# Starting a two-layer graph-attention and expert kernel: three first blocks interleaved, and no turn without a block between the layers

## The chip, the cores and the metric

One Trainium2 chip, one core of it. The metric is the device time of one execution in microseconds, as the median of several runs. All data are float32.

## The reference

Two layers follow each other. In each, the tokens x (128 graphs of 64 nodes with 256 features, 8192 tokens) go through graph attention inside each graph, and then through eight experts of which each token takes two:

```python
x = x + gnn(layernorm(x), adj)      # Wh = h @ W; e = Wh@a1 + (Wh@a2).T (layer 1: leaky)
                                    # softmax(where(adj > 0, e, -big)) @ Wh, then elu
x = x + experts(layernorm(x))       # top 2 of 8 by the router's logits
# layer 0: experts are 256 -> 256 (gelu) -> 256, and the normalised tokens are added too
# layer 1: experts are 256 -> 512 (relu) -> 256
```

In both layers a token's two expert outputs are weighted by a softmax over the two chosen logits.

## The kernel before

Tokens are cut into 16 blocks of 512 (four tiles of 128 tokens, two graphs each). For each layer and block there are two generators, whose pieces between two yields are called stages here.

- attend (L260 to L367, twelve stages): for layer 1 first the sum of block b's layer 0 results (L267: mid, plus the two expert rows yb of each token with their weights); layer normalisation's statistics (L223 to L233, with a power on GpSimd), its application on ScalarE (L240); transposes to xt (L251) with copies out of PSUM, one on VectorE (L255) and one on ScalarE (L257); the product with the weights (pw, L290), copied to wh by ScalarE (L297); scores (sm, pe), exponentials (L328), transposes of the attention (pp, L339, copied into one of three pT_bd), the product (po, L348) and the block's result xb (L362, L365).
- route (L402 to L513, ten stages): normalisation again (tn), transposes, logits (pl, L419), the largest two (L369 to L386, L445 to L450), weights, the positions of the tokens in the experts' lists (pn, L476; ix, L494), eight indirect writes of 512 token rows to the lists in DRAM (L499, GpSimd's queue), and from the third block of a part on a plan on VectorE (L535) that takes four slots.

A slot is 256 tokens of one expert. It is fetched from the list by SP's queue (xg, L611), its weights too (wc, L653 to L661; the biases come from a table bcat that is written at the start, L203 to L220), then transposed (x: px, L682), multiplied twice (h: ph, L751; y: py, L779), and its rows are scattered by indirect DMAs on GpSimd's queue, for layer 0 to res (L793), for layer 1 added into the output (L822). A part of a layer's blocks ends with every list filled up to whole slots (fill_up, L516) and a last plan of 15 slots. Layer 0 has two parts, so that layer 1 can begin when the first part's slots are done: blocks 0 to CUT - 1 (CUT is 10, L74) and the rest. The loads of a layer 1 block (L833 to L843) read mid and res, and the program lets them be issued only when all of that part's slots have had their y.

The order on SP, TensorE, VectorE and ScalarE is that of the program from L859 on, written out by hand; before that line, and on GpSimd, a scheduler decides. The loop at L894 makes one turn for each entry of blks: in turn t the attention of block t + 1, the routing of block t and four or five slots are interleaved stage by stage, and the first stages of block t + 2. At L861 blks has an empty entry between the layers: one turn attends to no block. Ahead of the loop stand the constants, the two layers' weights gw (L166 to L192: transposes, products with the score vectors, copies by VectorE), the router's weights, layer 0's bias table, the loads of three blocks and five stages. The loop begins with turn -1. Turn 1 makes layer 1's bias table, and turns 1 and 2 write pads into the unused ends of the lists (rest_of_lists, L846).

Of the kernel before, what the change touches and what calls it, by code (L numbers as in the profile page):

```python
# [8 lines left out]
F32 = mybir.dt.float32  # L9
# [7 lines left out]
P = 128  # L17
# [18 lines left out]
def adj_ffn_kernel(  # L36
# [37 lines left out]
    CUT = NB // 2 + 2  # L74
    CAP = N + 2 * SL
    SB = 2 * TB // SL
    LAG = 2
# [36 lines left out]

    ident = const.tile([P, P], F32, name="ident")
# [5 lines left out]
    for g in range(2):  # L121
        r = slice(g * NG, (g + 1) * NG)
        nc.gpsimd.memset(same[r, r], 1.0)
    before = const.tile([P, P], F32, name="before")
# [3 lines left out]
    nhalf = const.tile([P, TT], F32, name="nhalf")  # L128
    nc.gpsimd.memset(nhalf, -0.5)
# [13 lines left out]
    def counted(name, shape, pattern, base, mult):  # L143
        ti = work.tile(shape, I32, tag="adj", name=f"{name}_i")
        nc.gpsimd.iota(ti, pattern=pattern, base=base, channel_multiplier=mult)
        t = const.tile(shape, F32, name=name)
        nc.vector.tensor_copy(t, ti)
        return t

    token2 = counted("token2", [P, NT], [[2 * P, NT]], 0, 2)  # L150
    token = counted("token", [P, NT], [[P, NT]], 0, 1)
    place = counted("place", [P, ST], [[P, ST]], 0, 1)
    places = counted("places", [P, SL], [[1, SL]], 0, 0)
    steps = counted("steps", [P, KS], [[SL, KS]], 0, 0)
    snum = counted("snum", [P, SF], [[1, SF]], 0, 0)

# [4 lines left out]

# [4 lines left out]
    gw = []  # L166
    for l in range(2):
        gw.append(const.tile([P, KD, D + 2], F32, name=f"gw{l}"))
        av = const.tile([P, KD, 2], F32, name=f"av{l}")
# [3 lines left out]
        nc.sync.dma_start(out=av, in_=gnn_a[l])  # L173
        wt = work.tile([P, KD, D], F32, tag="xt", name=f"wt{l}", bufs=2)
        for o in range(KD):
# [5 lines left out]
            nc.vector.tensor_copy(wt[:, o, :], pt)  # L181
        for k in range(KD):
            pa = ps_c.tile([P, 2], F32, tag="a", name=f"pa{l}_{k}")
            for o in range(KD):
# [3 lines left out]
                    rhs=av[:, o, :],  # L188
# [3 lines left out]
            nc.vector.tensor_copy(gw[l][:, k, D : D + 2], pa)  # L192

    rw = []
    for l in range(2):
        t = const.tile([P, KD, E], F32, name=f"rw{l}")
        nc.sync.dma_start(out=t, in_=router[l].rearrange("(k p) e -> p k e", p=P))
        rw.append(t)
    gb2 = const.tile([P, 2, E], F32, name="gb2")
    nc.sync.dma_start(out=gb2[:, 0, :], in_=bg.partition_broadcast(P))  # L200
    nc.sync.dma_start(out=gb2[:, 1, :], in_=gbias.partition_broadcast(P))
# [43 lines left out]
    def transposed(src, tag, ptag, name):  # L245

        xt = work.tile([P, KD, TB], F32, tag=tag, name=f"xt_{name}", bufs=2)
        for k in range(KD):
# [5 lines left out]
            if k % 2 == 0:  # L254
# [591 lines left out]
    def rest_of_lists(l):  # L846

        for e in range(E):
# [3 lines left out]
                in_=pad[:, :, 0 : ROW[l]],  # L852
            )

    tb0 = gather_biases(0)

# [148 lines left out]
```

## Time and profile before

| | |
|---|---|
| median of 3 runs | 1488.62 us (1485.02 to 1490.95) |
| the profiled execution's own time | 1488.33 us |
| its span | 1486.6 us |
| busy: PE, PEld | 1275.2 us (86%), 1088.6 us (73%) |
| busy: DVE, ACT, POOL | 893.7, 661.6, 767.8 us |
| DMA | 315.42 MB, mean 212 GB/s |

PE is TensorE's matmuls, PEld its weight loads, DVE VectorE, ACT ScalarE, POOL GpSimd, SPq the DMA queue of SyncE. The busy slices give an engine's busy share in 40 equal parts of the span in tenths, PEclk the granted clock of TensorE. A line of the timeline has start and duration in us, engine, source line, operation and tiles, a count, and in brackets the idle time before it and what ended it. A line of busy time by stretch has the stretch, its length, and the busy time of PE, PEld, DVE, ACT and POOL (with the number of instructions), then the clock, the DMA share and GB/s.

### The profile page before, as it was taken

What the parts mean: (1) busy time and instruction counts of PE and PEld (TensorE: products, weight loads), DVE (VectorE), ACT (ScalarE), POOL (GpSimd) and SP (SyncE); (2) the same over time, 40 slices, a digit from 0 to 9 for tenths busy, and PEclk for the clock granted to TensorE, in tenths of its full rate; (3) what the DMA queues carried; (4) which work ended last, traced back from release to release, by engine and by line L of the source; (5) the groups of instructions that cost most, each with busy time, mean ns of one, the idle gap of its engine ahead of it and who ended that gap; (6) DMA issues with size and microseconds to landing.
All of it is one profiled execution on the core that took longest, in us unless ns stands there. A gap on an engine that the chain in (4) does not pass through costs nothing. (4 is left out here: it accounts for less than half of the span.)

```text
span 1486.6 us, 22819 instructions
## 1 busy us (share of the span) xinstructions
PE 1275.2 (86%) x6436; PEld 1088.6 (73%) x6436; DVE 893.7 (60%) x3418; ACT 661.6 (45%) x1549; POOL 767.8 (52%) x742
## 2 busy tenths in 40 slices
PE   4566899888889867888889988999889999899996
PEld 3454777777777755777778877788777887688985
DVE  3557777877667747666776666666666654423332
ACT  2443556554656523555544434445434443233332
POOL 3243566655666645355556545556455555534333
PEclk9676999998999979999999999999999999999999
DMA  4274676678676669667778877988778777998863
GB/s 125 87 224 145 197 234 210 219 250 246 214 225 212 217 229 285 206 227 233 255 253 231 231 193 208 268 227 223 208 210 232 199 196 205 239 248 214 225 174 60
DMA packets 267199, 315.42 MB, mean 212 GB/s; under 512 B 41404, under 2 KB 224319, under 8 KB 267073
## 3 DMA queue, kind: packets, MB, share of 16 engines
q1 hardware_dynamic: 222240, 227.80, 50.9%
q0 software_dynamic: 44832, 86.17, 22.1%
q8 instruction: 51, 0.84, 0.2%
q14 instruction: 76, 0.61, 0.1%
HBM read 215.03 MB, written 102.51 MB: 214 GB/s over the span
## 5 line engine op out<-in xcount | busy, mean ns | idle before, releaser
L751 PE MATMUL ph_s<-xT_s,wc_s 128*128 128x256 f32 x1760 | 417.2, 387 | 57.4 <-DVE xT_s L686 41.6
L779 PE MATMUL py_s<-wc_s,hT_s 128*128 128x256 f32 x1760 | 422.8, 391 | 21.7 <-issue 14.8
L751 PEld LDWEIGHTS ph_s<-xT_s,wc_s 128*128 128x128 f32 x1760 | 332.7, 192 | 119.2 <-DVE xT_s L686 57.4
L779 PEld LDWEIGHTS py_s<-wc_s,hT_s 128*128 128x128 f32 x1760 | 334.8, 195 | 68.8 <-issue 17.9
L822 POOL DMA_INDIRECT out_dram<-ys_s,to_s x142 | 223.5, 1574 | 304.9 <-ACT ys_s L819 189.9
L499 POOL DMA_INDIRECT lists<-tn_r,ix_r x256 | 249.6, 975 | 100.5 <-issue 66.3
L759 ACT ACTIVATE hT_s<-ph_s,wc_s 128x256 f32<-128x256 f32 x440 | 183.0, 469 | 184.6 <-issue 88.0
L793 POOL DMA_INDIRECT res<-ys_s,to_s x156 | 159.1, 1020 | 130.2 <-DVE ys_s L787 58.4
L787 DVE TENSOR_TENSOR ys_s<-py_s,wc_s 128x512 f32<-128x512 f32 x149 | 103.0, 691 | 187.4 <-PE py_s L779 182.7
L686 DVE COPY xT_s<-px_s 128x512 f32<-128x512 f32 x149 | 102.4, 687 | 118.3 <-PE px_s L682 118.3
L290 PE MATMUL pw_g<-gw,xt_g 128*128 128x258 f32 x512 | 130.5, 407 | 2.0 <-ACT xt_g L257 1.9
L290 PEld LDWEIGHTS pw_g<-gw,xt_g 128*128 128x128 f32 x512 | 98.6, 202 | 25.6 <-ACT xt_g L257 9.5
L819 ACT ACTIVATE ys_s<-ys_s,cf_s 128x256 f32<-128x256 f32 x142 | 64.1, 498 | 117.7 <-DVE ys_s L787 117.4
L240 ACT ACTIVATE xn_g<-xs,nb_g,rs_g 128x256 f32<-128x256 f32 x128 | 66.4, 589 | 85.5 <-DVE nb_g L238 85.5
L240 ACT ACTIVATE tn_r<-xb_g,nb_r,rs_r 128x256 f32<-128x256 f32 x128 | 66.4, 589 | 70.4 <-DVE nb_r L238 70.4
L682 PE MATMUL px_s<-ident,xg_s 128*128 128x128 f32 x596 | 91.6, 277 | 0.0
L682 PEld LDWEIGHTS px_s<-ident,xg_s 128*128 128x128 f32 x596 | 76.0, 146 | 13.4 <-issue 0.8
L232 POOL TENSOR_TENSOR rs_r<-ve_r,nhalf 128x4 f32<-128x4 f32 x32 | 39.4, 1232 | 86.8 <-DVE ve_r L230 43.8
L348 PE MATMUL po_g<-wh_g,pT_bd 128*128 128x256 f32 x256 | 71.1, 426 | 9.7 <-ACT pT_bd L342 9.5
L339 PE MATMUL pp_g<-ident,ee_g 128*64 128x128 f32 x128 | 22.1, 302 | 61.1 <-DVE ee_g L335 41.0
L297 ACT COPY wh_g<-pw_g 128x258 f32<-128x258 f32 x128 | 48.0, 375 | 59.1 <-PE pw_g L290 58.2
L348 PEld LDWEIGHTS po_g<-wh_g,pT_bd 128*128 128x128 f32 x256 | 52.6, 213 | 23.3 <-ACT pT_bd L342 10.9
(475 smaller groups left out, 1626.3 us busy)
## 6 DMA issues: line engine op xcount, KB each, us to landing
wc_s<-in_w_dram SPq DMA_DIRECT2D x142, 512.0 KB, 4.6
wc_s<-in_w_dram SPq DMA_DIRECT2D x156, 256.0 KB, 3.4
xg_s<-lists SPq DMA_DIRECT2D x78, 258.0 KB, 4.1
xg_s<-lists SPq DMA_DIRECT2D x71, 260.0 KB, 4.3
yb<-res SPq DMA_DIRECT2D x16, 1024.0 KB, 11.1
wc_s<-bcat SPq DMA_DIRECT2D x78, 129.0 KB, 3.9
wc_s<-bcat SPq DMA_DIRECT2D x71, 130.0 KB, 6.2
xs<-in_x_dram SPq DMA_DIRECT2D x16, 512.0 KB, 5.6
```

The source lines that it names most:

```text
L240: nc.scalar.activation(outs(t), xb[:, t, :], AF.Identity, bias=nb[:, t : t + 1], scale=rs[:, t : t + 1])
L290: nc.tensor.matmul(pw, lhsT=xt[:, k, t * P : (t + 1) * P], rhs=gw[l][:, k, :], start=(k == 0), stop=(k == KD - 1),)
L348: nc.tensor.matmul(po[h][:, j, :], lhsT=pT[:, 2 * h + j, :], rhs=wh[:, 2 * h + j, 0:D], start=True, stop=True,)
L499: ins = nc.gpsimd.indirect_dma_start(out=lists[l], out_offset=bass.IndirectOffsetOnAxis(ap=ix[:, k, t : t + 1], axis=0), in_=tn[:, t, 0 : ...
L682: nc.tensor.transpose(px[:, c, t * P : (t + 1) * P], xg[:, t, c * P : (c + 1) * P], ident)
L686: nc.vector.tensor_copy(xT, px)
L751: nc.tensor.matmul(ph[:, j, :], lhsT=wc[:, o : o + P], rhs=xT[:, c, :], start=(c == 0), stop=(c == KD - 1),)
L759: nc.scalar.activation(hT[:, f + j, :], ph[:, j, :], AF.Gelu if l == 0 else AF.Relu, bias=wc[:, OB1[l] + f + j : OB1[l] + f + j + 1],)
L779: nc.tensor.matmul(py[:, t, :], lhsT=hT[:, f, t * P : (t + 1) * P], rhs=wc[:, O2[l] + f * D : O2[l] + (f + 1) * D], start=(f == 0), stop=( ...
L787: nc.vector.tensor_tensor(ys, py, wc[:, OB2[l] : OB1[l]].unsqueeze(1).to_broadcast([P, ST, D]), ALU.add)
L793: ins = nc.gpsimd.indirect_dma_start(out=res[sl["part"]], out_offset=self.row(sl, t), in_=ys[:, t, :], in_offset=None, bounds_check=2 * N - 1,
L822: ins = nc.gpsimd.indirect_dma_start(out=out, out_offset=self.row(sl, t), in_=ys[:, t, :], in_offset=None, compute_op=ALU.add,)
```

## The change

Five things are changed. (1) The hand-written order starts ahead of the constants. SP's queue begins with the first block's x, then gw and the score vectors of layer 0; the rest of the first three blocks' loads and the router's weights follow. Layer 1's gw, layer 0's bias table and the counted constants come at fixed places in a new list of rounds. The copies in make_gw are ScalarE's. (2) In these rounds the attention and routing of blocks 0, 1 and 2 advance side by side, one stage of each in a round; block 3 joins in round 11 and block 4, with its first three stages, in round 20. For blocks 0 to 2 both copies of the transposes are ScalarE's. (3) The loop begins at turn 3. Layer 1's bias table and the pads now stand in turns 3 and 4. (4) blks has no empty entry. The load of layer 1's block 0 stands at the end of the turn two ahead of the boundary; its first stage (the sum), which would come early in the next turn, is left out there and comes together with the second, later in that turn. (5) CUT is 9. The number of slots is the same: 43 and 35 for layer 0's two parts where there were 47 and 31, and 71 for layer 1. The index of pT_bd follows from the missing entry.

```diff
     NB = N // TB
-    CUT = NB // 2 + 2
+    CUT = NB // 2 + 1
     CAP = N + 2 * SL
     SB = 2 * TB // SL
+    FIRST = 3
     LAG = 2
...
+
+    ctx.enter_context(tc.manual_schedule(engines=ORDERED))
     ident = const.tile([P, P], F32, name="ident")
...
-    def counted(name, shape, pattern, base, mult):
-        ti = work.tile(shape, I32, tag="adj", name=f"{name}_i")
-        nc.gpsimd.iota(ti, pattern=pattern, base=base, channel_multiplier=mult)
-        t = const.tile(shape, F32, name=name)
-        nc.vector.tensor_copy(t, ti)
-        return t
-
-    token2 = counted("token2", [P, NT], [[2 * P, NT]], 0, 2)
-    token = counted("token", [P, NT], [[P, NT]], 0, 1)
-    place = counted("place", [P, ST], [[P, ST]], 0, 1)
-    places = counted("places", [P, SL], [[1, SL]], 0, 0)
-    steps = counted("steps", [P, KS], [[SL, KS]], 0, 0)
-    snum = counted("snum", [P, SF], [[1, SF]], 0, 0)
-
...
-    gw = []
-    for l in range(2):
+    gw, av = [], []
+
+    def load_gw(l):
         gw.append(const.tile([P, KD, D + 2], F32, name=f"gw{l}"))
-        av = const.tile([P, KD, 2], F32, name=f"av{l}")
+        av.append(const.tile([P, KD, 2], F32, name=f"av{l}"))
         nc.sync.dma_start(
...
         )
-        nc.sync.dma_start(out=av, in_=gnn_a[l])
+        nc.sync.dma_start(out=av[l], in_=gnn_a[l])
+
+    def make_gw(l):
         wt = work.tile([P, KD, D], F32, tag="xt", name=f"wt{l}", bufs=2)
...
                 )
-            nc.vector.tensor_copy(wt[:, o, :], pt)
+            nc.scalar.copy(wt[:, o, :], pt)
         for k in range(KD):
...
                     lhsT=wt[:, o, k * P : (k + 1) * P],
-                    rhs=av[:, o, :],
+                    rhs=av[l][:, o, :],
                     start=(o == 0),
...
                 )
-            nc.vector.tensor_copy(gw[l][:, k, D : D + 2], pa)
-
-    rw = []
-    for l in range(2):
-        t = const.tile([P, KD, E], F32, name=f"rw{l}")
-        nc.sync.dma_start(out=t, in_=router[l].rearrange("(k p) e -> p k e", p=P))
-        rw.append(t)
+            nc.scalar.copy(gw[l][:, k, D : D + 2], pa)
+
+    rw = [const.tile([P, KD, E], F32, name=f"rw{l}") for l in range(2)]
     gb2 = const.tile([P, 2, E], F32, name="gb2")
-    nc.sync.dma_start(out=gb2[:, 0, :], in_=bg.partition_broadcast(P))
-    nc.sync.dma_start(out=gb2[:, 1, :], in_=gbias.partition_broadcast(P))
+
+    def load_router():
+        for l in range(2):
+            nc.sync.dma_start(out=rw[l], in_=router[l].rearrange("(k p) e -> p k e", p=P))
+        nc.sync.dma_start(out=gb2[:, 0, :], in_=bg.partition_broadcast(P))
+        nc.sync.dma_start(out=gb2[:, 1, :], in_=gbias.partition_broadcast(P))
+
+    def counted(name, shape, pattern, base, mult):
+        ti = work.tile(shape, I32, tag="cap", name=f"{name}_i")
+        nc.gpsimd.iota(ti, pattern=pattern, base=base, channel_multiplier=mult)
+        t = const.tile(shape, F32, name=name)
+        nc.vector.tensor_copy(t, ti)
+        return t
...
-    def transposed(src, tag, ptag, name):
+    def transposed(src, tag, ptag, name, both):
...
                 )
-            if k % 2 == 0:
+            if k % 2 == 0 and not both:
                 nc.vector.tensor_copy(xt[:, k, :], pt)
...
         yield
-        xt = transposed(xn, "xt", "a", name)
+        xt = transposed(xn, "xt", "a", name, l == 0 and b < FIRST)
         yield
...
             nc.tensor.transpose(pp[:, t, :], ee[:, t, :], ident)
-        pT = pT_bd[(NB * l + b + l) % 3]
+        pT = pT_bd[(NB * l + b) % 3]
         nc.vector.tensor_copy(pT[0:NG, :, 0:NG], pp[:, :, 0:NG])
...
         yield
-        tT = transposed(tn, "tT", "r", name)
+        tT = transposed(tn, "tT", "r", name, l == 0 and b < FIRST)
         yield
...
-    def load_block(l, b):
+    def load_block(l, b, first=None):
...
         nc.sync.dma_start(out=xs, in_=(mid_t if l else x_t)[b])
+        if first:
+            first()
         if l:
...
-    tb0 = gather_biases(0)
-
...
-
-    ctx.enter_context(tc.manual_schedule(engines=ORDERED))
     slots = Slots()
-    blks = [{"l": 0, "b": b} for b in range(NB)] + [{}] + [{"l": 1, "b": b} for b in range(NB)]
+    blks = [{"l": l, "b": b} for l in range(2) for b in range(NB)]
...
-    def load(i):
+    def load(i, first=None):
         if there(i):
...
                 assert all(s["l"] or s["part"] != part(k["b"]) for s in slots.all[slots.ny :])
-            k["in"] = load_block(k["l"], k["b"])
+            k["in"] = load_block(k["l"], k["b"], first)
             k["a"] = attend(k["l"], k["b"], k)
...
     h, y, x = slots.h, slots.y, slots.x
-    load(0)
+
+
+    load(0, lambda: load_gw(0))
     load(1)
-    put_biases(0, tb0)
     load(2)
-    a(0, 3)
+    load_router()
+    a(0, 2)
+    make_gw(0)
+    a(0)
     a(1, 2)
-    for t in range(-1, len(blks)):
+    token2 = counted("token2", [P, NT], [[2 * P, NT]], 0, 2)
+    token = counted("token", [P, NT], [[P, NT]], 0, 1)
+    place = counted("place", [P, ST], [[P, ST]], 0, 1)
+    att = lambda b: [(a, b)] * 9 + [(a, b, 2), (a, b)]
+    chains = [
+        (0, att(0)[3:] + [(r, 0)] * 10),
+        (1, att(1)[2:] + [(r, 1)] * 10),
+        (2, att(2) + [(r, 2)] * 10),
+        (11, att(FIRST) + [(r, FIRST)] * 2),
+        (20, [(a, FIRST + 1)] * 3),
+    ]
+    turn = 0
+    while any(c for _, c in chains):
+        for first, chain in chains:
+            if turn >= first and chain:
+                stage, *what = chain.pop(0)
+                stage(*what)
+        if turn == 2:
+            places = counted("places", [P, SL], [[1, SL]], 0, 0)
+            steps = counted("steps", [P, KS], [[SL, KS]], 0, 0)
+            snum = counted("snum", [P, SF], [[1, SF]], 0, 0)
+            tb0 = gather_biases(0)
+        if turn == 5:
+            put_biases(0, tb0)
+            load_gw(1)
+        if turn in (6, 8, 11):
+            load(FIRST + (turn - 6) // 2)
+        if turn == 11:
+            make_gw(1)
+        turn += 1
+    slots.fetch()
+    for t in range(FIRST, len(blks)):
         n = t + 1
         more = slots.nf - slots.ny > SB or len(slots.all) - slots.ny > SB
-        if t >= 0 and t + 3 != NB + 1:
+        if t + 3 != NB:
             load(t + 3)
-        if t == 1:
+        if t == FIRST:
             put_biases(1, gather_biases(1))
             rest_of_lists(0)
-        if t == 2:
+        if t == FIRST + 1:
             rest_of_lists(1)
...
         r(t)
-        if t >= 0:
+        if t + 2 != NB:
             a(t + 2)
...
         y()
-        if t >= 0:
-            a(t + 2)
+        a(t + 2, 1 + (t + 2 == NB))
         if more:
...
         r(t)
-        if t + 3 == NB + 1:
+        if t + 3 == NB:
             load(t + 3)
```

More of the change, by code (lines that the diff above doesn't have):

```diff
@@ L123, in adj_ffn_kernel @@
         nc.gpsimd.memset(same[r, r], 1.0)
+    nhalf = const.tile([P, TT], F32, name="nhalf")
+    nc.gpsimd.memset(nhalf, -0.5)
     before = const.tile([P, P], F32, name="before")
@@ L127, in adj_ffn_kernel @@
     nc.gpsimd.memset(ones, 1.0)
-    nhalf = const.tile([P, TT], F32, name="nhalf")
-    nc.gpsimd.memset(nhalf, -0.5)
     order = const.tile([P, E], F32, name="order")
```

## The prediction

> **What bounds the kernel now.** I read the page's slices first, then the chain that ended last, then busy time in stretches cut where TensorE (it runs in program order) starts a block's first transposes (tile pt_g): 44.1, 69.0, 95.7, 122.8, 150.0, 182.9 us for blocks 1 to 6 of layer 0, then every 31 to 35 us. I call such a stretch a turn.
>
> ```profile
> PE   4566899888889867888889988999889999899996
> PEclk9676999998999979999999999999999999999999
> ```
>
> TensorE is at eight or nine tenths except in the first four slices (150 us), where its granted clock is low too, and in slices 15 and 16 (520 to 595 us), at the boundary of the layers. The chain that ended last has PE products back to back from about 1290 us on:
>
> ```profile
> 1364.09 3.45 PE ph_s L751 x16
> 1368.82 3.46 PE py_s L779 x16
> ```
>
> So the end is a run of expert products without a gap, and their sum is the same in both kernels. A gain can only be TensorE's idle or slow time ahead of it. The stretches (PE, PEld, DVE, ACT, POOL busy, clock, DMA share, GB/s):
>
> ```profile
> 44.10:69.00 24.90, 16.27 (x68) 12.21 (x68) 13.63 (x53) 11.62 (x31) 4.06 (x5) 0.71 0.18 53
> 69.00:95.70 26.70, 17.65 (x68) 13.15 (x68) 15.11 (x63) 11.72 (x31) 11.94 (x13) 0.69 0.81 235
> 95.70:122.80 27.10, 18.04 (x68) 13.38 (x68) 15.24 (x63) 11.78 (x31) 11.84 (x13) 0.69 0.55 166
> ...
> 244.90:275.60 30.70, 27.30 (x150) 23.25 (x149) 24.03 (x96) 17.56 (x40) 18.36 (x20) 1.00 0.71 229
> 444.00:478.60 34.60, 31.35 (x170) 26.80 (x169) 25.54 (x99) 20.97 (x44) 21.25 (x22) 1.00 0.66 206
> 511.30:556.70 45.40, 31.20 (x133) 25.26 (x132) 22.10 (x89) 13.54 (x26) 22.57 (x23) 0.77 0.73 239
> 556.70:597.00 40.30, 30.03 (x142) 24.74 (x141) 27.96 (x96) 16.86 (x35) 21.78 (x23) 0.96 0.98 281
> 597.00:635.70 38.70, 32.68 (x170) 27.70 (x169) 25.70 (x86) 19.37 (x41) 14.43 (x15) 0.96 0.67 212
> 796.60:841.50 44.90, 40.76 (x215) 35.62 (x214) 29.30 (x113) 19.84 (x51) 24.63 (x21) 1.00 0.82 223
> ```
>
> The first three are turns of the start: 25 to 27 us each, 8 to 9 of them idle, clock 0.7: one block after the other, a chain of short steps and no expert product to fill it. Then a layer 0 turn with four expert slots (30.7), with five (34.6): a slot more costs 3.9 us. From 511.3 to 556.7 is the turn without a block: 45.4 us, 31.2 busy, clock 0.77. 556.7 is the turn in which layer 0's last list is filled up (40.3 with no routing in it), 597.0 an ordinary layer 1 turn with five layer 0 slots (38.7), 796.6 one with four layer 1 slots (44.8). In the turn without a block the timeline has this:
>
> ```profile
> 530.19 3.89 DVE L267 SCALAR_TENSOR_TENSOR xs<-yb,cs,xs 128x256 f32<-128x256 f32 x8 [5.87 <-DMA yb<-res]
> 534.74 3.78 PE L779 MATMUL py_s<-wc_s,hT_s 128*128 128x256 f32 x8 [6.52 <-DVE ys_s L787]
> ```
>
> VectorE stands 5.87 us for the landing of layer 1 block 0's yb at the sum L267, then sums for 3.89 us; TensorE gets its next product 6.52 us late and runs it in 3.78 us for 8 matmuls instead of 1.89: its clock has dropped.
>
> [...] L290's 16 matmuls take 5.09 us in the turn at 44.1 and 3.83 at 341.0. [...] finished products wait behind L267 above. So a step placed too early in an engine's order stalls what is behind it, and so will three interleaved chains. [...] The list writes (L499) here land 2.6 to 2.8 us after issue.
>
> **The change, part A: the start.** The order of the built program gives the same slot products done at block 6's first transposes of layer 0 (4), so I compare that moment: 182.9 us before. Added work: nothing on TensorE; 6 copies of 0.69 us of the three blocks and 4 weight copies leave VectorE for ScalarE (0.59 us there), which has room (12 of 27 us busy per turn).
>
> What follows is an estimate. I walked the new order by hand, each step starting when its input and its engine's step before are done, with the trace's durations: statistics 2.3, pow on GpSimd 1.04, normalising 2.1, transposes 2.8 with their wait, pw 3.8 warm to 5.1 cold (I take 4.3), pe 1.1, exponentials 1.4, po 2.0 to 3.7 (2.9), largest 1.3, second largest 1.7, pn and positions 2.7. x now stands first in SP's queue: it lands at about 5 us (13.4 before), its normalising starts at 8.9 (18.5 before). From there chain 0 has its pw at 12.6 to 17.0, exponentials to 24.1, pT at 29.5 (behind block 2's xn on ScalarE), po 30.3 to 33.0, xb at 36.3, statistics to 41.1, tn 45.3 to 47.4 (behind block 2's exponentials), largest at 52.7, second largest at 58.6, pn at 70.7 (in TensorE's order behind block 3's transposes, which wait for its xn), positions (ix) at 73. Alone it is hardly earlier than before (70.7) although it starts ten sooner. But ix of block 1 comes at 83 (97 before) and of block 2 at 91 (124).
>
> Next late is GpSimd. Its order has 8 list writes for each of three blocks and one mid write ahead of the pow of blocks 4 and route 3, and it issues one write in 1.27 us:
>
> ```profile
> 98.81 1.10 POOL L499 DMA_INDIRECT lists<-tn_r,ix_r  x1 [0.28 <-DMA lists<-pad]
> 100.22 0.98 POOL L499 DMA_INDIRECT lists<-tn_r,ix_r  x1 [0.30 <-issue]
> ```
>
> 25 issues after 73 end at 73 + 31.5 = 104.5, the two pows at 106.6; VectorE, with block 2's plan (22 steps of 0.2) and statistics, reaches the same point at 104.3. Block 4's transposes: 106.5, against 122.8. That is 16 us gained.
>
> Part of it goes back. The pads, the second biases and layer 1's bcat stood in turns without slots; now they stand in SP's queue between the first list reads and the first expert weights:
>
> ```profile
> 66.27 1.22 SPq L214 DMA_DIRECT2D tb<-in_b_dram  x1
> 72.90 0.39 SPq L220 DMA_DIRECT2D bcat<-tb  x1
> 92.46 6.03 SPq L850 DMA_DIRECT2D lists<-pad  x8
> ```
>
> List reads from 107 (last write lands) take 3.6 us, xs and adj 1, tb to its landing 7.2 (65.7 to 72.9 above), eight pads 6.0, the first slot's weights 2.1 and landing 5: about 132.5. TensorE would be at the first slot's ph at 106.5 + 21.5 (block 4's po ends so long after its pt_g) = 128. The wait of 4.5 us, cold matmuls after it, two slots and their activations (block 5's xn stands behind them on ScalarE) make this turn 38 us; bounds 30 (weights in time) to 41. The next, with two slots, 28.5 (27.2 with none; 32.8 with four as the first such turn). Block 6: 106.5 + 38 + 28.5 = 173, so A = 9 to 10 us. I take 9. Bounds: 20 if matmuls are warm and weights in time; 0 if matmuls stay cold and the weights come later still.
>
> **Part B: the boundary.** From block 10 of layer 0 (306.4 us; 20 slots done in both) to block 9 of layer 1 (932.9; 94 done in both) before takes 626.5 us. CUT at 9 moves the fill-up one turn earlier at the same cost (37.6 against 30.7 in the turn at 337.1). It makes the turns after it five-slot turns one block sooner; the number of slots stays 78 for layer 0 (43 + 35 for 47 + 31). After: the fill-up turn 37.6; blocks 11 to 15 with five slots 5 x 34.6 = 173.0; layer 1 block 0, now with route 15 and five slots, 38.7; block 1 with the second fill-up 38.7 + 5 = 43.7 (the penalty was 6.9 at 337.1 and some 4 at 556.7); blocks 2 to 4 3 x 38.7 = 116.1; block 5 with one layer 1 slot among five 38.7 + 3.3 = 42.0; blocks 6 to 8 with five layer 1 slots where there were four, 3 x (44.8 + 7.2) = 156.0 (7.2: 3.45 + 3.46 us of products in the chain, and 0.3 of transposes not overlapped). One turn in four had 1.7 more. Sum 608.8. B = 626.5 - 608.8 = 17.7, I take 18. That is the idle of one turn fewer and the stall with its cold matmuls. Cross-check by what goes and comes: 45.4 goes; one more layer 0 slot in a turn (3.9), three more layer 1 slots (21.6) and the fill-up beside a block (3.4) come, 3.1 leave with block 5's turn (42.0 for 45.1): 19.6, less the 1.7.
>
> The sum L267 of block 0 now stands after two products and most of a turn's steps, some 20 us behind its load; yb took 9.8 to 14.9 us to land over the sixteen. I cost it at its 3.9 us alone; with the cover gone it costs 6 to 9 again: behind it on VectorE stand the next xT and ys, and TensorE and GpSimd wait for those. Moving nhalf and the constants, pT_bd's index and the load callbacks cost nothing: GpSimd's memsets end before 7 us, ahead of its first pow. The tail after block 9 has the same order: 0.
>
> **Sum.** The profiled execution took 1488.3 us (span 1486.6, 1.7 around it; the median of the runs is 1488.6, so the same). 1488.3 - 9 - 18 = 1461.
>
> **Rivals.** (1) The start gives more: interleaving keeps TensorE warm and the first weights come in time, A = 20 to 28: 1442 to 1450. For: from 18 to 45 us my walk has PE nearly without gaps. Against: the SP queue above. (2) The start gives nothing: three chains in one FIFO order hold each other up, and GpSimd's 25 issues start at 83: A = -1 to 0, 1471. With part of B lost as well (VectorE stands at L267 again, 6 to 9 us), 1478. For: VectorE is busy only 15 of 27 us before, so rounds are latency, not work. (3) Slower: with five layer 1 slots a turn and no empty turn, yb lands late in every layer 1 turn, 5.87 us of standing and 3 of cold matmuls each as at 530: over nine turns 80, so 1541; it ends slower than before from four such turns on. Against: bytes per us stay (229 GB/s with four slots) and only one of sixteen loads was late before. (4) The empty turn's removal is no gain, as its slots only move: B = 3, A = 9: 1476.
>
> **Chances.** Forecast with A 0 to 20 and B 9 to 21 (1447 to 1479): 0.72. Rival 1: 0.12; 2: 0.09; 4: 0.04; 3: 0.03. Bounds of A and B hardly fall together, so the range is 1445 to 1477, with under 2 in 10 outside (half of rival 1 and of 2, rival 3, the forecast's ends). A measurement tells about 0.5% (7.4 us) from no change; faster by that, below 1481: 0.94 (the forecast and rivals 1, 2 and 4 but their outermost end); same 0.03; slower 0.03 (rival 3).
>
> **What would show it.** Right: block 4's first transposes at 100 to 112 us, gated by rs_g after block 2's list writes; TensorE's first ph waiting for a DMA of wc near 132; block 6 near 173; no DMA wait at the sum L265 (its line after); block 9 of layer 1 some 27 us earlier than 932.9, and the rest equal. Wrong: positions of block 0 after 83 or before 65; a yb wait in turns of layer 1; a five-slot layer 1 turn over 54 us.

## The result, and the profile after

| | before | after |
|---|---|---|
| median of four runs each | 1487.43 us (1485.02 to 1490.95) | 1467.71 us (1464.47 to 1469.72) |
| ratio, with its 95% interval | | 0.9863 (0.9847 to 0.9879) |
| profiled execution, its span | 1488.33, 1486.6 us | 1464.47, 1462.6 us |

The kernel became 1.4% faster: about 20 us by the medians, 24 in the two profiled executions (the profiled one of after is the fastest of its four). The forecast was 1461 with 1445 to 1477: inside the range, with 7 us less gained. Eight of the twelve runs below fell on chips on which the kernel before itself takes 1713 to 1715 us instead of 1487, so their ratios are to the kernel before on their own chip.

The page's slices of the kernel after:

```profile
PE   6646789889989888888889999899988998899996
PEclk9766999989999999999999999999999999999999
```

The dip at slices 15 and 16 is gone. The first four (146 us) still stand at 4 to 6 tenths, with a clock of 7, 6 and 6 tenths from the second on. Busy time by stretch, cut where a block's first transposes start (PE, PEld, DVE, ACT, POOL, clock, DMA share, GB/s):

```profile
9.81:72.06 62.25, 45.37 (x180) 33.75 (x181) 33.20 (x123) 33.91 (x89) 15.04 (x20) 0.82 0.31 88
72.06:111.28 39.22, 18.55 (x77) 14.74 (x77) 23.07 (x117) 12.45 (x33) 26.93 (x28) 0.63 0.27 95
111.28:150.05 38.77, 27.49 (x113) 20.88 (x114) 17.39 (x67) 16.02 (x38) 5.67 (x7) 0.70 0.94 280
150.05:177.16 27.11, 19.27 (x110) 16.24 (x109) 20.35 (x83) 13.17 (x33) 18.01 (x19) 0.97 0.66 213
177.16:210.60 33.44, 30.27 (x148) 24.91 (x149) 24.64 (x103) 20.15 (x44) 17.74 (x19) 0.92 0.61 193
444.60:479.20 34.60, 31.35 (x171) 26.80 (x170) 25.39 (x99) 20.95 (x44) 20.85 (x22) 1.00 0.62 198
479.20:519.70 40.50, 33.59 (x171) 28.40 (x170) 28.91 (x107) 20.96 (x44) 23.14 (x24) 0.92 0.78 263
519.70:557.20 37.50, 31.23 (x170) 26.66 (x169) 29.24 (x108) 21.33 (x45) 22.71 (x24) 1.00 0.81 262
557.20:598.10 40.90, 34.81 (x170) 29.31 (x169) 32.51 (x127) 19.36 (x41) 22.16 (x23) 0.92 0.92 276
755.40:806.60 51.20, 48.13 (x251) 42.01 (x249) 30.46 (x118) 23.46 (x58) 24.75 (x21) 1.00 0.78 227
```

Line by line: the three interleaved blocks (62 us, 45 of them busy); block 3, of which TensorE works only 18.55 of 39.22 us; the turn of block 4 with the first slots; that of block 5; block 6; a five-slot turn (34.6, as before); the turn of layer 0's block 15, 40.5; layer 1's blocks 0 and 1; and a turn with five layer 1 slots (51.2; the forecast had 52.0). Two comparisons, each of one profile of either kernel, show where the time went. At block 6 of layer 0 the same slots are done in both kernels: 177.2 us for 182.9. From block 10 of layer 0 (302.9) to block 9 of layer 1 (909.0) are 606.1 us for 626.5. So the boundary gave 20.4, and the start 5.7 at block 6 and 3.4 at block 10 (302.9 for 306.4). After block 9 both take the same. The start's share did not repeat in the later profiles, as will be seen.

The start, in SP's queue (start, duration, idle in brackets):

```profile
110.99 3.07 SPq L609 DMA_DIRECT2D xg_s<-lists  x4
115.72 2.26 SPq L212 DMA_DIRECT2D tb<-in_b_dram  x1
123.15 0.40 SPq L218 DMA_DIRECT2D bcat<-tb  x1
123.65 9.29 SPq L850 DMA_DIRECT2D lists<-pad  x8
134.15 0.40 SPq L651 DMA_DIRECT2D wc_s<-in_w_dram  x1
143.06 6.41 SPq L850 DMA_DIRECT2D lists<-pad  x8
166.40 5.08 SPq L609 DMA_DIRECT2D xg_s<-lists  x4
```

GpSimd's queue and TensorE in the same stretch:

```profile
77.72 1.11 POOL L497 DMA_INDIRECT lists<-tn_r,ix_r  x1 [5.26 <-DVE cs L466]
79.13 0.98 POOL L497 DMA_INDIRECT lists<-tn_r,ix_r  x1 [0.30 <-issue]
...
108.36 0.96 POOL L497 DMA_INDIRECT lists<-tn_r,ix_r  x1 [0.30 <-issue]
109.34 1.05 POOL L230 TENSOR_TENSOR rs_g<-ve_g,nhalf 128x4 f32<-128x4 f32 x1
110.37 1.00 POOL L230 TENSOR_TENSOR rs_r<-ve_r,nhalf 128x4 f32<-128x4 f32 x1
```

```profile
111.28 2.80 PE L249 MATMUL pt_g<-ident,xn_g 128*128 128x128 f32 x8 [13.60 <-ACT xn_g L238]
...
128.47 3.78 PE L346 MATMUL po_g<-wh_g,pT_bd 128*128 128x256 f32 x8 [1.84 <-ACT pT_bd L340]
138.66 3.38 PE L749 MATMUL ph_s<-xT_s,wc_s 128*128 128x256 f32 x8 [6.40 <-DMA wc_s<-in_w_dram]
```

25 writes follow each other from 77.72 to 109.3 without a break, then come the two pows, and block 4's first transposes had waited 13.60 us for the xn that hangs on the first pow. The list reads at 110.99 are followed by the tables and eight pads that take 9.29 us to issue, and only then by the first weights at 134.15. TensorE had ended block 4's po at 132.25: its first expert product waited 6.40 us and took 3.38 us for eight matmuls, at a granted clock of 0.56 from 138.66 to 141.87; the next two, at 143.25 and 145.09, took 1.99 and 1.89 us at a clock of 1.00. The second eight pads stand in the next turn.

The boundary: the sum (L265) of layer 1's block 0, VectorE and TensorE.

```profile
498.82 3.75 DVE L265 SCALAR_TENSOR_TENSOR xs<-yb,cs,xs 128x256 f32<-128x256 f32 x8
...
504.81 0.68 DVE L684 COPY xT_s<-px_s 128x512 f32<-128x512 f32 x1
505.55 3.78 PE L749 MATMUL ph_s<-xT_s,wc_s 128*128 128x256 f32 x8 [4.90 <-DVE xT_s L684]
```

No line on the sum has a DMA wait any more, in any of the sixteen blocks. But the sum and the statistics behind it keep VectorE for 6 us, the next xT copy stands right behind them, and TensorE waits 4.90 us for it and runs the product in 3.78, at a granted clock of 0.50. Block 15's turn is 40.5 us long where its five-slot neighbours take 34.6.

### The profile page after: what moved, and what is told of

It reads as the page before. It is cut to its first block, busy times and chain, and to the rows that moved or that the text cites. A ratio compares the mean times of both kernels' runs of the same rounds, so it can differ in the third digit from the quotient of the medians.

```text
span 1462.6 us, 22822 instructions
## 1 busy us (share of the span) xinstructions
PE 1264.9 (86%) x6436; PEld 1082.9 (74%) x6436; DVE 885.6 (61%) x3404; ACT 670.3 (46%) x1567; POOL 767.8 (52%) x742
## 5 line engine op out<-in xcount | busy, mean ns | idle before, releaser
L777 PE MATMUL py_s<-wc_s,hT_s 128*128 128x256 f32 x1760 | 417.1, 387 | 14.9 <-issue 14.6
L777 PEld LDWEIGHTS py_s<-wc_s,hT_s 128*128 128x128 f32 x1760 | 331.4, 193 | 59.9 <-issue 17.2
L817 ACT ACTIVATE ys_s<-ys_s,cf_s 128x256 f32<-128x256 f32 x142 | 64.1, 499 | 141.1 <-DVE ys_s L785 134.8
L288 PE MATMUL pw_g<-gw,xt_g 128*128 128x258 f32 x512 | 125.5, 395 | 1.7 <-ACT wh_g L295 1.3
L277 POOL TENSOR_SCALAR cap_g<-adj 128x256 f32<-128x256 int32 x32 | 35.7, 1117 | 91.6 <-DMA adj<-in_adj_dram 90.2
L417 PEld LDWEIGHTS pl_r<-rw,xt_r 128*128 128x128 f32 x512 | 68.1, 207 | 2.9 <-DVE xt_r L253 0.6
```

The source lines that it names most:

```text
L288: nc.tensor.matmul(pw, lhsT=xt[:, k, t * P : (t + 1) * P], rhs=gw[l][:, k, :], start=(k == 0), stop=(k == KD - 1),)
L777: nc.tensor.matmul(py[:, t, :], lhsT=hT[:, f, t * P : (t + 1) * P], rhs=wc[:, O2[l] + f * D : O2[l] + (f + 1) * D], start=(f == 0), stop=( ...
```

## Experiments on chips where the kernel before takes 1487 us

These four ran on one chip with seven runs of the kernel before: 1487.66 us.

**The changed kernel once more.** No edit.

> The changed kernel itself, unchanged, beside the earlier experiments. There the kernel before took 1714 us, and from block 5 on each turn showed TensorE idle for 4 to 10 us while GpSimd wrote list rows and SP read lists. Theory (that idle hits turns with a block and five slots hardest, so the turn taken away is paid back): the boundary alone was at 1.007 of the kernel before, the start alone at 0.999, so both together at 1.003 to 1.007. Rival (the 0.986 of the first measurement holds wherever it is taken, and the edits of the two halves were at fault): 0.986.

1469.21 us, ratio 0.9875 (0.9855 to 0.9896): the first result holds in a second set of runs. The rival's number came; its second half, that the edits of the two halves were at fault, is not tested by it, and neither is the theory, which was about chips of the other kind. Its start is slower than in the first profile though. Same program, same place:

```profile
143.27 3.78 PE L749 MATMUL ph_s<-xT_s,wc_s 128*128 128x256 f32 x8 [11.69 <-DMA wc_s<-in_w_dram]
```

A wait of 11.69 us instead of 6.40. The first weights were issued at 135.46 for 134.15, and the median time from issue to landing of the weights in this stretch was 7.1 us for 4.1. Block 6 came at 182.6, block 10 at 308.9. Block 10 to block 9 of layer 1: 606.7, the same as in the first profile (606.1).

**The sum in three pieces.**

```diff
                         ALU.mult,
                         ALU.add,
                     )
+                if b == 0 and t == 1:
+                    yield
...
-        a(t + 2, 1 + (t + 2 == NB))
+        a(t + 2)
...
         h()
+        if t + 2 == NB:
+            a(NB)
...
         x()
+        if t + 2 == NB:
+            a(NB)
```

> The changed kernel with the sum of layer 1 block 0 and its statistics in three pieces spread over block 15's turn instead of one piece of 6.2 us. Theory (the piece as a whole keeps VectorE from the next xT, TensorE waits 4.9 us for it and runs the next product cold): that wait goes and block 15's turn is 4 to 6 us shorter than the changed kernel's in the same conditions, 0.3% of the time. Rival (the pieces only move the wait to other products): the turn within 1.5 us.

1465.24 us, ratio 0.9851 (0.9830 to 0.9872); its four runs (1463.1 to 1466.1) lie below the four of the unchanged kernel (1467.2 to 1470.9). Block 15's turn takes 37.8 us for 41.3, and block 10 to block 9 is 602.7 us.

```profile
502.71 1.91 DVE L265 SCALAR_TENSOR_TENSOR xs<-yb,cs,xs 128x256 f32<-128x256 f32 x4
504.54 0.68 DVE L686 COPY xT_s<-px_s 128x512 f32<-128x512 f32 x1
505.27 1.95 DVE L265 SCALAR_TENSOR_TENSOR xs<-yb,cs,xs 128x256 f32<-128x256 f32 x4
505.28 1.99 PE L751 MATMUL ph_s<-xT_s,wc_s 128*128 128x256 f32 x8 [0.74 <-DVE xT_s L686]
```

The xT copy now lies between the two halves of the sum, and the product behind it waits 0.74 us and takes 1.99 us for its eight matmuls, where in the first profile of the changed kernel it took 3.78, behind 4.90 us of idle and at a clock of 0.50. The theory is right in kind, and the rival (within 1.5 us) is out; 3.5 us are won instead of 4 to 6. The rest of the turn's excess (37.8 for 34.6) is in part 1.79 us in which a later product waits for its weights.

**Pads early, block 3 and block 4 sooner.**

```diff
-        (11, att(FIRST) + [(r, FIRST)] * 2),
-        (20, [(a, FIRST + 1)] * 3),
+        (7, att(FIRST) + [(r, FIRST)] * 2),
+        (13, [(a, FIRST + 1)] * 3),
...
             put_biases(0, tb0)
+            tb1 = gather_biases(1)
             load_gw(1)
+            rest_of_lists(0)
+            rest_of_lists(1)
+            put_biases(1, tb1)
...
-        if t == FIRST:
-            put_biases(1, gather_biases(1))
-            rest_of_lists(0)
-        if t == FIRST + 1:
-            rest_of_lists(1)
```

> The changed kernel with the pads and layer 1's biases ahead of block 3's load in the start, block 3's chain four rounds sooner and block 4's seven. The earlier runs showed two things: pads just ahead of the list writes hold those up by 6.5 us, and it is the pow of route 3, not only that of block 4, that stands behind the list writes. Theory (these two gates, GpSimd's list writes and SP's pads, set the start): list writes start at 76 to 80, block 4's first transposes stand ahead of 100, the first expert product is at 122 to 127 instead of 138.7, and block 6 is 11 to 16 us earlier than in the changed kernel in the same conditions. Rival (three chains already fill VectorE and ScalarE, so block 3 in their midst delays the first three): list writes after 84, block 6 less than 5 us earlier.

1465.39 us, ratio 0.9852 (0.9830 to 0.9874); the intervals of this run and of the unchanged kernel overlap. Block 6 is at 178.0 for 182.6, 4.6 us sooner. Both numbers of the rival came and none of the theory's (block 4's first transposes are at 107.1, the first expert product at 140.95); of the theory only its second gate, SP's queue, was as it said. GpSimd, VectorE, then TensorE:

```profile
93.92 1.11 POOL L497 DMA_INDIRECT lists<-tn_r,ix_r  x1 [1.15 <-DVE ix_r L492]
...
116.31 0.16 DVE L236 SCALAR_TENSOR_TENSOR nb_r<-mv_r,rs_r 128x4 f32<-128x4 f32 x1 [5.97 <-POOL rs_r L230]
...
123.20 5.62 PE L288 MATMUL pw_g<-gw,xt_g 128*128 128x258 f32 x16 [14.15 <-DVE xt_g L253]
...
137.62 3.49 PE L346 MATMUL po_g<-wh_g,pT_bd 128*128 128x256 f32 x8 [2.00 <-ACT pT_bd L340]
140.95 1.89 PE L749 MATMUL ph_s<-xT_s,wc_s 128*128 128x256 f32 x8
```

The list writes start at 93.92, 16 us later: block 3 among the first three delays them, as the rival said (block 4's statistics, sooner too, may have a part in it). Block 4's product pw then waits 14.15 us, since its xt copy (122.37) stands on VectorE behind route 3's normalisation, which waits 5.97 us for a pow that GpSimd does between list writes, and behind block 2's plan (118.64 to 122.4). But the first expert product, at 140.95, follows po without any wait for weights: without pads and tables in between, the first weights are issued 6.9 us after the last list write ends, where the unchanged kernel on this chip takes 26.3. In spite of list writes 16 us later that product comes 2.3 us sooner.

**List reads one by one.**

```diff
             self.limit = self.nf
+            self.reads()
+
+        def reads(self):
             while self.nf < min(len(self.all), self.ny + 8):
...
             self.ahead()
+            self.reads()
```

> The changed kernel with list reads issued one after each slot's second product instead of five together at a turn's end. Theory (TensorE's idle of 4 to 10 us a turn comes where SP's burst of list reads meets GpSimd's list writes; layer 1 block 1 of the start-alone run, without list writes, had none): the idle shrinks by half or more, 26 turns x 4 to 8 us, 100 to 200 us less than the changed kernel in the same conditions. Rival (the list writes alone do it, or the weights' reads): within 20 us.

1468.87 us, ratio 0.9876 (0.9857 to 0.9895): no difference. It was made against the idle time that the other chips showed (below); on this chip that idle is absent (TensorE's gaps of over 3 us from block 5 to block 9 of layer 1 add up to 13.8 us in the unchanged kernel, where the start-alone run below has 142), so it says only that the burst of five reads costs nothing here. Block 6 at 179.8, block 10 to block 9 607.3 us.

## Experiments on chips where the kernel before takes 1714 us

**The boundary alone.** The kernel before with CUT at 9, no empty entry, and the later sum:

```diff
-    CUT = NB // 2 + 2
+    CUT = NB // 2 + 1
...
-        pT = pT_bd[(NB * l + b + l) % 3]
+        pT = pT_bd[(NB * l + b) % 3]
...
-    blks = [{"l": 0, "b": b} for b in range(NB)] + [{}] + [{"l": 1, "b": b} for b in range(NB)]
+    blks = [{"l": 0, "b": b} for b in range(NB)] + [{"l": 1, "b": b} for b in range(NB)]
...
-        if t >= 0:
+        if t >= 0 and t + 2 != NB:
             a(t + 2)
...
-            a(t + 2)
+            a(t + 2, 1 + (t + 2 == NB))
```

> The kernel before with the boundary's part alone (no turn without a block, CUT at 9, the sum of layer 1 block 0 later). Theory (the two parts are separate, and the boundary carried most of the gain: 20.4 us of 24 in the traces): 1468 us, that is 20 below the kernel before; block 10 of layer 0 still near 306, block 9 of layer 1 near 912, and the turn of block 15 near 40 us with a late product in it. Rival (the parts need each other, since a layer's turns only stay full when the start runs ahead): under 14 us gained.

> The kernel before with the boundary's part alone, once more on another chip if there is one. Theory (the parts are separate, the boundary carries 20.4 of 24 us): ratio to the kernel before 0.986 to 0.987; block 10 of layer 0 near 306, block 9 of layer 1 near 912, and a wait of TensorE of 4 to 6 us in the turn of block 15. Rival (the parts need each other): ratio 0.991 or more.

> The kernel before with the boundary's part alone, on a chip where the kernel before takes 1487 us if this one is such. Theory (the boundary carries 20 us of the gain and the start 0 to 4): ratio 0.985 to 0.989, block 10 of layer 0 near 306, block 9 of layer 1 near 911, a wait of 4 to 6 us for VectorE's xT in block 15's turn. Rival (the parts need each other): ratio 0.991 or more.

Three chips: 1.0065 (1.0045 to 1.0085), 1.0071 (1.0053 to 1.0090), 1.0049 (1.0030 to 1.0068). The boundary alone is slower there, by 9 to 11 us, and the theory missed three times. The rival's number is met, but its reason has no support: with a start beside it, the run with block 4's pow moved (below, its start no faster) is at 1.0041, still slower, and the best kernel with both parts is at 0.9969 there, not at 0.986. The changed kernel itself was not run on these chips. Whether the boundary alone gives its 20 us where the kernel before takes 1487 was not measured either; there it was always run with the start.

**The start alone.** The changed kernel with CUT at 10, the empty entry and the sum's old place put back (the lines above the other way).

> The changed kernel with the turn without a block, CUT at 10 and the sum's old place put back: the start alone. Theory: it gives 3 to 4 us, 1484 to 1485; block 6 near 177 and block 10 near 303. Rival (the start gives the 9 us of the forecast, and the boundary less): 1479. Rival (the start gives nothing and costs, hidden by the boundary): 1488 or more.

0.9988 (0.9968 to 1.0008): at most 5.5 us gained, with zero inside the interval. That leaves room for the theory's 3 to 4 and for nothing, and on this chip not for the forecast's 9. Beside the boundary-alone run on the same chip, which has the old start, block 6 comes later (190.5 for 187.0) and block 10 sooner (350.8 for 355.0).

**Why the boundary costs there.** In the start-alone run, layer 1's block 1 and block 3, TensorE with SP and GpSimd:

```profile
716.90 3.83 PE L288 MATMUL pw_g<-gw,xt_g 128*128 128x258 f32 x16
717.78 3.90 SPq L609 DMA_DIRECT2D xg_s<-lists  x5
```

```profile
796.01 0.96 POOL L497 DMA_INDIRECT lists<-tn_r,ix_r  x1 [0.30 <-issue]
797.20 6.08 SPq L609 DMA_DIRECT2D xg_s<-lists  x5
...
807.33 4.20 PE L288 MATMUL pw_g<-gw,xt_g 128*128 128x258 f32 x8 [7.68 <-issue]
```

In block 1's stretch, right after the turn without a block, no list is written, five list reads take 3.90 us to issue and pw's sixteen matmuls run through; the stretch takes 37.5 us. In block 3's, list writes and list reads meet, the reads take 6.08 us, and pw stands still for 7.68 us in its middle; the stretch takes 48.7. Turns with both show gaps of 3.4 to 9.8 us: from block 5 to block 9 of layer 1, TensorE's gaps of over 3 us add up to 142 us in this run, to 13 in the changed kernel's first profile. The turn without a block is what makes the one stretch without list writes; taking it away takes the one cheap stretch away. In the first profile of before the same stretch has no list writes either, but is not cheap there (38.7 us, the next two 38.7 and 39.4). No run varied it alone, so it is argued, not shown, and it can be only part of the cause. By stretches, in us, with the start-alone and the boundary-alone run of one chip on the right (from block 10 on those two differ in the boundary's edits alone):

| stretch | before, after (1487) | start alone, boundary alone (1714) |
|---|---|---|
| block 10 to block 15 of layer 0 | 172.3, 176.2 | 222.5, 230.5 |
| block 15 to block 2 of layer 1 | 157.1, 119.0 | 177.6, 150.2 |
| block 2 to block 6 of layer 1 | 160.9, 157.2 | 201.2, 202.4 |
| block 6 to block 9 of layer 1 | 136.2, 153.7 | 152.0, 176.9 |
| sum | 626.5, 606.1 | 753.4, 760.0 |

Where the turn is taken away the gain is 27.4 us instead of 38.1; the missing 10.7 are about the cheap stretch (37.5 for 48.7). But the three turns that now do five layer 1 slots instead of four cost 24.9 more instead of 17.5, and the other two rows together lose 9.2 where they lose 0.2 on the 1487 us side. So the loss of the one turn's gain is spread over all stretches, and why fuller turns cost more on these chips stays open.

**Pads in the rounds.** The changed kernel; pads and tables stand in round 11 of the start instead of turns 3 and 4.

```diff
         if turn == 11:
             make_gw(1)
+            put_biases(1, gather_biases(1))
+            rest_of_lists(0)
+            rest_of_lists(1)
```

> The changed kernel with the pads of both lists and layer 1's biases moved from the first two turns into the rounds of the start, ahead of the list writes. Theory (SP's queue sets the first expert weights, as it holds tb, bcat and 16 pads between the first list reads and the first weights): the first weights are issued near 118 instead of 134, the wait of 6.4 us ahead of the first ph goes, and with it the late list reads of the next turn: block 6 at 167 to 171 instead of 177, 1458 to 1462 us. Rival (GpSimd's 25 list writes set it, and TensorE then only waits for the next link): block 6 stays within 2 us of 177 and the time within 2 of the changed kernel.

0.9995 (0.9969 to 1.0020). GpSimd's first list write, and TensorE at block 4's end:

```profile
84.22 1.11 POOL L497 DMA_INDIRECT lists<-tn_r,ix_r  x1 [11.84 <-DMA lists<-pad]
...
134.96 3.55 PE L346 MATMUL po_g<-wh_g,pT_bd 128*128 128x256 f32 x8 [1.84 <-ACT pT_bd L340]
138.35 1.89 PE L749 MATMUL ph_s<-xT_s,wc_s 128*128 128x256 f32 x8
```

The weights are issued at 122.52 for 136.03 in the start-alone run (whose start is the changed kernel's) and no product waits for them: block 6 is at 181.7 for 190.5. The theory's 6 to 10 us are there, and its rival is out; in time it cannot be read off, as the changed kernel was not run beside it (the run below with block 4's pow moved, its block 6 at 191.5, took 7.9 us more). But the first list write waited 11.84 us for the pads that now stand just ahead of it, and started at 84.22 instead of 77.22. Part of the delay had moved.

**Block 4's pow ahead of the writes.**

```diff
-        (20, [(a, FIRST + 1)] * 3),
+        (17, [(a, FIRST + 1)] * 3),
```

> The changed kernel with block 4's statistics three rounds sooner, so that its pow stands ahead of block 2's list writes on GpSimd. Theory: block 4's first transposes come at 101 to 104 instead of 111, but the first expert product still waits for its weights near 137, so that the 8 us are given back in the same turn: block 6 within 2 us of 177, 1465 to 1468. Rival (the pow is the link that sets the whole start): block 6 at 169, 1459.

1.0041 (1.0023 to 1.0058), block 6 at 191.5 for 190.5 in the start-alone run: the theory's result came, the rival's did not. But most of the gain was given back at another place than the theory had. TensorE, then VectorE:

```profile
103.36 1.71 PE L249 MATMUL pt_g<-ident,xn_g 128*128 128x128 f32 x8 [3.10 <-DVE xb_g L360]
114.32 1.23 PE L288 MATMUL pw_g<-gw,xt_g 128*128 128x258 f32 x2 [9.25 <-DVE xt_g L253]
...
142.05 3.78 PE L749 MATMUL ph_s<-xT_s,wc_s 128*128 128x256 f32 x8 [7.87 <-DMA wc_s<-in_w_dram]
```

```profile
113.43 0.16 DVE L236 SCALAR_TENSOR_TENSOR nb_r<-mv_r,rs_r 128x4 f32<-128x4 f32 x1 [2.15 <-POOL rs_r L230]
...
113.58 0.68 DVE L253 COPY xt_g<-pt_g 128x512 f32<-128x512 f32 x1
```

Block 4's transposes start at 103.36 for 115.2, and are of no use: pw waits 9.25 us for the xt copy. In VectorE's order that copy stands behind block 2's plan and route 3's statistics, which keep VectorE until 111.28, and then behind route 3's normalisation, whose pow still comes after the last list write (112.35). The wait for that pow is only 2.15 us; the rest is VectorE's own work. By po 10.6 of the 11.9 us are gone (130.40 for 131.65 in the start-alone run). At the end of the turn the first product waits 7.87 us for weights.

**Both.** The two edits above together.

> The changed kernel with both: the pads and layer 1's biases in the rounds of the start, and block 4's statistics three rounds sooner. Read against the changed kernel's share of the kernel before, 0.986. Theory (two gates in series: block 4's pow behind the list writes, and the first weights behind the pads; each alone is partly given back to the other): block 4's first transposes at 101 to 104, the first weights issued near 118, block 6 at 162 to 167 instead of 177, and 10 to 14 us less than the changed kernel: a ratio to the kernel before of 0.977 to 0.980. Rival (the start is bound by something later, such as cold products or ScalarE): block 6 above 172, ratio 0.984 or more.

1.0019 (1.0005 to 1.0034), first transposes of block 4 at 109.1, first product at 140.4 without a wait for weights, block 6 at 188.2. The theory of two gates in series fell: the pads delay the first list write (83.5), and block 4's pow now stands behind the list writes of blocks 0 and 1. VectorE stands 10.18 us for that pow, with block 2's positions behind it, so that the last list writes and route 3's pow (118.2) come later too, and pw waits 9.05 us much as before.

**Pads early, and the sum in pieces.** The pads and tables as in the run with the chains moved, but the chains left where they were; the sum in three pieces.

> The changed kernel with two edits: pads and layer 1's biases early in the start (ahead of block 3's load, so that they land some 30 us before the first list writes), the chains as they were; and the sum of layer 1 block 0 in three pieces. Theory (SP's pads set the first weights: the wait of 6.4 to 11 us ahead of the first expert product was theirs; with them just ahead of the list writes they only moved their delay there): list writes start at 76 to 79 as in the changed kernel, the first weights are issued at 115 to 119, the first expert product runs at 131 to 134 with no DMA wait (138.7 and 143.3 before), block 6 is at 168 to 173 (177.2 and 182.6), and with the 4 us of the pieces the ratio to the kernel before is 0.977 to 0.982. Rival (something else is late by then, ScalarE's or VectorE's order): block 6 above 176 and a ratio of 0.984 or more, what the pieces alone gave.

0.9969 (0.9952 to 0.9985): on these chips the only one of six kernels that is faster than before. SP and TensorE:

```profile
118.27 0.38 SPq L653 DMA_DIRECT2D wc_s<-in_w_dram  x1
...
133.33 3.61 PE L348 MATMUL po_g<-wh_g,pT_bd 128*128 128x256 f32 x8 [1.85 <-ACT pT_bd L342]
136.78 1.89 PE L751 MATMUL ph_s<-xT_s,wc_s 128*128 128x256 f32 x8
```

The list writes start at 77.3, the first weights are issued at 118.27 for 136.03, the first product follows po directly at 136.78 for 141.1, and block 6 is at 181.5 for 190.5 in the start-alone run. That run is of another chip; with the old start block 6 comes at 186.4 on this chip and at 187.0 on that one. Of the theory, the list writes and the weights came as it said; the product (131 to 134), block 6 and the ratio were forecast from the other chips and did not come here, and the rival's numbers, from there too, decide nothing. The wait for weights belongs to the pads and tables. Its time where the kernel before takes 1487 us was not measured; if the 9 us and the 3.5 of the pieces carry over, it would be about 1457 (1469.2 - 9 - 3.5), an estimate.

## Why the prediction was right or wrong

**The total** lies in the range because part B carried it: by the medians 19.7 and 18.5 us were gained, 19 to 20 of them at the boundary. Part A gave next to nothing, and the range took that in by its lower bound.

**Part B was right, and a little low.** Forecast 626.5 to 608.8, measured 606.1, 606.7 and 607.3 in three profiles, beside one profile of before. Terms: the fill-up turn 37.8 (37.6), four five-slot turns 34.6 (34.6), layer 1's block 0 37.5 (38.7), block 1 40.9 (43.7), block 5 41.2 (42.0), blocks 6 to 8 51.2 each (52.0). One term was too low: the last five-slot turn, of block 15, took 40.5 for 34.6. The step that failed there is "I cost it at its 3.9 us alone": on VectorE, in front of an xT, 3.75 us of sum and 2.4 of statistics cost TensorE 5.9. The pieces showed it by winning 3.5 of them back. That the sum of the terms still came within 3 us is in part luck: the terms that were too high are some 9 us together, the allowance of 1.7 included.

**Part A was wrong in size: 9 forecast, 0 to 6 measured at block 6.** In the four profiles with this start and the 1487 us kernel beside them, block 6 came at 177.2, 182.6, 181.0 and 179.8 (180.2 on average, for 182.9 in the one profile of before) and block 10 at 302.9, 308.9, 307.0 and 305.6 (306.1 for 306.4). On average the start gave 3 us at block 6 and nothing at block 10. By its own steps, in the first profile:

| step | forecast | measured |
|---|---|---|
| block 0's normalising, pw | 8.9, 12.6 to 17.0 | 9.2, 12.4 to 17.5 |
| po, pn of block 0 | 30.3 to 33.0, 70.7 | 32.4 to 36.0, 74.7 |
| first list write, last pow | 73, 106.6 | 77.7, 111.4 |
| block 4's first transposes | 106.5 | 111.3 |
| first weights landed | 132.5 | 138.7 |
| turn of block 4, of block 5 | 38, 28.5 | 38.8, 27.1 |
| block 6 | 173 | 177.2 |

Three terms were mis-sized. The first is the walk along the chain: it was 2 us short by po and 4 by pn, where products ran at a lower clock (pl of block 0 took 3.42 us at a granted clock of 0.50; those at 121.71 and 161.19 took 1.85 at 1.00). GpSimd's 25 writes took 31.6 us (31.5) and the link to block 4 was as forecast, so block 4's first transposes came at 111.3 on average of the four profiles, 4.8 us late; in the first profile that is all that is missing at block 6. The second is "a wait of 4.5 us", bounds 30 to 41 for that turn. (Its terms add up to 131.9, not 132.5; that changes nothing.) The pads took 9.29 us to issue where I had 6.0 from before, and the weights 4.1 to 7.1 us to land; the waits were 6.4, 11.7, 9.0 and 10.4 us in the four profiles, and the turn 38.8 to 44.3, 41.7 on average for 38. The turn of block 5 gave 1.4 back (27.1 for 28.5). That pads and tables together make the wait is shown: with them early or in the rounds no first product waited for weights, in four kernels, and from the end of the last list write to the issue of the first weights passed 6.8 to 9.8 us, where it is 24.8 to 27.7 with them in between. How much of it is the tables', no run separates. The third is block 6's turn, 33.4 to 34.0 for 31.3: in the first profile it begins after 5.20 us of idle and with a product of 3.29 us at a clock of 0.57 (the next, at 187.46, takes 1.89), and it takes 2.4 us of what was left; the forecast had compared at block 6 and looked no further.

**Rivals.** (2), the start gives nothing, was nearer to the truth than my forecast: its 1471 is 2 to 3 us from the medians 1467.7 and 1469.2, my 1461 is 7 to 8, though not by its mechanism, as GpSimd's issues start at 77.7, not 83. (1) and (4) are out: no A of 20, and B is 20, not 3. (3) is out where the kernel before takes 1487 us: no sum waits for yb. On the other chips the boundary alone is slower, and turns with five layer 1 slots do cost more there (59.0 for 50.7 us, three of them), but no sum waits for yb in those runs either: it is another mechanism, which I did not think of.

**The signs.** Block 4's first transposes at 100 to 112 behind the last pow: yes. The first ph waiting for wc near 132: yes, but longer. Block 6 near 173: no, 177.2 and later. No DMA wait at the sum: yes. Block 9 of layer 1 some 27 us earlier: less, 23.9, and 17.3 in the second profile.

## What to carry to other kernels

Work that leaves a quiet stretch goes into a queue with something behind it: ask what stands behind it there (pads ahead of the first weights, with a wait of 6.40 us for those; a sum ahead of an xT, with one of 4.90), and give it the place where nothing does. Starting a chain sooner helped here only as far as each engine on its way got past the same gate: moving one pow brought block 4's transposes 11.9 us sooner and left the copy behind VectorE's other work and another pow, so that pw waited 9.25 us for it. And a gain that one profile shows in a start with loads on its path should be seen in several profiles before it is believed: here block 6 was reached at 177.2 to 182.6 us by the same start.

## What the hardware showed unexpectedly

In five sets of runs the same kernel before took 1487 us (two sets) or 1713 to 1715 (three, each on another chip). In the slower profiles single instructions last as long as in the others (px 0.60 us at a granted clock of 1.00, xT 0.68, GpSimd's list write 0.96), but in many turns in which GpSimd's list writes and SP's list reads overlap, results of TensorE are taken up 5 to 11 us late by ScalarE and VectorE: in the run with the pads in the rounds px is recorded at 481.99 and its copy at 493.11, where the changed kernel's own profile has 413.40 and 414.03. SP's five list reads take 6.42 us to issue there for 4.70. Where the delay arises isn't settled; single list reads, meant against it, were only run where it is absent.
